# Sums of rows and edge products kept in PSUM, and pass 0's gathered rows copied there by ACT, in a graph network kernel

## The chip, the cores and the metric

The kernel runs on one core of one Trainium2 chip. The metric is the device time of one execution in microseconds; the figure for the kernel before is the median of three runs. Times that name a line come from one profiled execution of the kernel before.

The engines are named as in the profile: PE is TensorE, DVE is VectorE, ACT is ScalarE, POOL is GpSimd, and SP is SyncE, which here only issues DMAs. PEld is PE's loading of weights.

## The reference, cut to what matters

Two layers of a graph network over 6250 nodes with 256 features and 100000 edges. The edges are sorted by their destination. Everything is fp32.

```python
# layer 0
theta_x = (x[dst] - x[src]) @ theta_w.T + theta_b
phi_x   = x[src] @ phi_w.T + phi_b
out = segment_max(relu(theta_x + phi_x), dst)           # 0 where a node has no edge
x = layernorm(x + out)
# layer 1
hv = x @ W_in + b_in
for W, b in ((W_u0, b_u0), (W_u1, b_u1)):
    m   = relu(concatenate([hv[src], he], -1) @ W + b)    # he: 64 features per edge
    msg = segment_max(m, dst)
    hv  = where(has_in, msg + hv, hv)
x = layernorm(x + relu(hv @ W_ro + b_ro))
```

The theta term of x[dst] is the same for all edges of a node, so the maximum over the edges of a node needs only one row per edge that depends on the source. In layer 0 that row is x[src] @ (phi - theta); in layer 1 it is hv[src] @ W (upper part) plus he @ W (lower part).

## The kernel before, in words

A prologue in `gnn_kernel` makes the table of source rows of layer 0 in DRAM (L533 on PE, L536 on ACT). It also works out, in `check`, whether the destinations are sorted. They are, so the program takes the branch `in_order`.

`in_order` calls `sweep(r)` three times: pass 0 is layer 0, and passes 1 and 2 are the two rounds of layer 1. The edges lie in 17 blocks; in a block, each of the 128 partitions holds a run of consecutive edges (56 in most blocks). One step `s` handles one edge per partition, 128 edges, and a pass has `FS` = 782 steps. In each step:

- `sources` (L719, POOL) gathers the 128 source rows of 1 KB each from `table[r]` into a slice of the tile `run`, which holds K = 8 steps and has four buffers. It is issued 16 steps ahead (`AHEAD`).
- In passes 1 and 2, `pair` (L730, PE) multiplies the edge features of two steps by the lower part of the weights: two matrix products of 128x512 fp32 into one PSUM bank `hp`, one pair of steps ahead. Every second step the addition L923 (DVE) adds this bank to the two gathered rows in `run`. The edge features come by `features`, a DMA of ACT's queue every eight steps.
- L926 (DVE, `scalar_tensor_tensor`) carries the running maximum: the previous row, cut by `lim` where a new destination begins, against the current row, in place in `run`. A block's first row has no predecessor and is left as it is.
- Every eight steps SP stores the finished `run` tile to the DRAM tensor `S` (L932).

At the end of a block `over_lanes` carries the maxima from partition to partition: PE transposes (L741), ACT copies (L739, L758) and a DVE scan (L746).

A node's result is the row of `S` at its last edge, with what earlier partitions carry. This is done for tiles of 128 nodes, 49 in each pass, by `node(t, g, b)`. It is cut into small functions that `at` hangs on steps, called slots here. For each tile: `rows` gathers the rows of `S` (L771, POOL), `picks` (L783, DVE) and `carried` (L790, PE) bring what is carried. In pass 0 `theta` multiplies the tile of x (L700 and L702, PE, with the bank tag "he") at slot 8t+20, `theta_out` (L801, ACT) copies the product out at slot 8t+21, and `first_a` to `first_i` do the relu (L810, ACT), the layernorm (L682 is its square root, on ACT), the transposes (L692, PE, and their copy `aT`, L694, ACT), the products for the next pass and their copies (L830 and L834, ACT). Passes 1 and 2 have `next_a` to `next_d` and `last_d` to `last_g` at these places.

In the first part of pass 0 `count(c)` counts the edges of each node, at slot 3c+4 for c = 0 to 97: DVE compares the lower seven and the upper bits of the destinations of eight steps with a row of indices, which makes the one-hots `ol` (L647) and `oh` (L650), and PE multiplies them into `hist` (L653). The node stage of pass 0 begins when this is done, at slot 297.

The order on each engine is the order of the program text (`manual_schedule`): an engine executes its instructions in that order, and each waits for the data and buffers that it needs. [...]the tags "v", "pr", "he" and "tp" have two each.

Of the kernel before, what the change touches and what calls it, by code (L numbers as in the profile page):

```python
# [8 lines left out]
F32 = mybir.dt.float32  # L9
BF16 = mybir.dt.bfloat16  # L10
I32 = mybir.dt.int32
AF = mybir.ActivationFunctionType
OP = mybir.AluOpType
# [4 lines left out]
P = 128  # L18
N = 6250
D = 256  # L20
DE = 64
E = 100000
NT = 49
K = 8
# [12 lines left out]
FS = sum(BLOCKS)  # L37
# [396 lines left out]
def gnn_kernel(  # L434
# [3 lines left out]
    nc = tc.nc  # L438
    const = ctx.enter_context(tc.tile_pool(name="const", bufs=1))
# [32 lines left out]
    fd, pd, ld, nd = (ends_sb[:, i, :] for i in range(4))  # L472
    s_s = const.tile([P, FS], I32)
    whole = const.tile([P, NB], F32)
    lim = const.tile([P, FS], F32)
    breaks = const.tile([P, 1], I32)
    lo = const.tile([P, FS], BF16)
    hi = const.tile([P, FS], BF16)
    with tc.manual_schedule(), tc.tile_pool(name="pro", bufs=2) as pro, \
            tc.tile_pool(name="pro_ps", bufs=4, space=PSUM) as pps:  # L480
        wd = pro.tile([P, 2, D], F32, name="wd", bufs=1)
        wt = pro.tile([P, 2, D], F32, name="wt", bufs=1)
        nc.sync.dma_start(wd, ph_wT.rearrange("(k p) f -> p k f", p=P))
        nc.scalar.dma_start(wt, th_wT.rearrange("(k p) f -> p k f", p=P))
        dp = pro.tile([P, 2 * FS], I32, name="dp", bufs=1)
        d_s, p_s = dp[:, :FS], dp[:, FS:]
        parts = []
        for g in range(NT // PART):
            xg = pro.tile([P, 2, PART * P], F32, name="xg", bufs=NT // PART)
            nc.sync.dma_start(xg, xTn[:, :, g * PART * P:(g + 1) * PART * P])  # L490
            parts.append(xg)
            if g == 0:
                nc.sync.dma_start(dp, pos[:, 4 * NB:4 * NB + 2 * FS])
                nc.sync.dma_start(ends_sb.rearrange("p a b -> p (a b)"), pos[:, :4 * NB])
        nc.sync.dma_start(s_s, pos[:, 4 * NB + 2 * FS:])
        nc.vector.tensor_sub(wd, wd, wt)

        def check():
            down = pro.tile([P, FS], F32, name="down", bufs=1)
            nc.vector.tensor_tensor(down, p_s, d_s, OP.is_gt)  # L500
            downs = pro.tile([P, 1], F32, name="downs", bufs=1)
            nc.vector.tensor_reduce(downs, down, AX.X, OP.max)
            out_of = pro.tile([1, 2, NB], F32, name="out_of", bufs=1)
            nc.vector.tensor_tensor(out_of[:, 0, :], fd[0:1, :], floor, OP.is_lt)
            nc.vector.tensor_tensor(out_of[:, 1, :], fd[0:1, :], ceil, OP.is_gt)
            bad = pro.tile([1, 1], F32, name="bad", bufs=1)
            nc.vector.tensor_reduce(bad, out_of.rearrange("p a b -> p (a b)"), AX.X, OP.max)
            nc.vector.tensor_max(downs[0:1, :], downs[0:1, :], bad)
            breaks_p = pps.tile([P, 512], F32, name="breaks_p", bufs=1)
            nc.tensor.matmul(breaks_p[:, :1], every, downs, start=True, stop=True)  # L510
            nc.vector.tensor_copy(breaks, breaks_p[:, :1])
            keep = pro.tile([P, FS], F32, name="down", bufs=1)
            nc.vector.tensor_tensor(keep, p_s, d_s, OP.is_equal)
            alike = BLOCKS.count(BLOCKS[0])
            nc.vector.tensor_reduce(whole[:, :alike], keep[:, :alike * BLOCKS[0]].rearrange(
                "p (b s) -> p b s", s=BLOCKS[0]), AX.X, OP.min)
            for b in range(alike, NB):
                nc.vector.tensor_reduce(whole[:, b:b + 1], keep[:, FIRST[b]:FIRST[b] + BLOCKS[b]], AX.X, OP.min)
            nc.vector.tensor_scalar(lim, keep, 2.0 * BIG, -BIG, OP.mult, OP.add)
            bits = pro.tile([P, FS], I32, name="bits", bufs=1)  # L520
            nc.vector.tensor_scalar(bits, d_s, P - 1, None, OP.bitwise_and)
            nc.vector.tensor_copy(lo, bits)
            nc.vector.tensor_scalar(bits, d_s, 7, None, OP.arith_shift_right)
            nc.vector.tensor_copy(hi, bits)

        for g, xg in enumerate(parts):
            g0 = pro.tile([P, PART, D], F32, name="g0", bufs=3)
            for i in range(0, PART, 2):
                w = min(2, PART - i)
                ps = pps.tile([P, 512], F32, name="ps0")  # L530
                for q in range(w):
                    for k in range(2):
                        nc.tensor.matmul(ps[:, q * D:(q + 1) * D], xg[:, k, (i + q) * P:(i + q + 1) * P], wd[:, k, :],  # L533
                                         start=(k == 0), stop=(k == 1))
                put = g0[:, i:i + w, :].rearrange("p a f -> p (a f)")
                nc.scalar.copy(put, ps[:, :w * D])  # L536
            nc.sync.dma_start(table[0][g * PART * P:(g + 1) * PART * P, :].rearrange("(a p) f -> p a f", p=P), g0)
            if g == 0:
                check()
# [10 lines left out]
def in_order(ctx: ExitStack, tc: tile.TileContext, g):  # L550
# [5 lines left out]

    nc = tc.nc
    table, ident, above, every, col, col_f = (g[n] for n in ("table", "ident", "above", "every", "col", "col_f"))
    whole, lim, lo, hi, s_s, fd, pd, ld, nd = (g[n] for n in ("whole", "lim", "lo", "hi", "s_s", "fd", "pd", "ld", "nd"))
    heT, xTn, xn, out = (g[n] for n in ("heT", "xTn", "xn", "out"))  # L560
    ctx.enter_context(tc.manual_schedule())
    one = ctx.enter_context(tc.tile_pool(name="one", bufs=1))
# [75 lines left out]
        nc.vector.tensor_add(tb, tb, pb)  # L638


    hist = psum.tile([P, 512], F32, tag="v", name="hist")

    def count(c):
        k = min(K, FS - c * K)
        cut = slice(c * K, c * K + k)
        ol = work.tile([P, K, P], BF16, name="ol", bufs=1)
        nc.vector.tensor_tensor(ol[:, :k, :], col.unsqueeze(1).to_broadcast([P, k, P]),  # L647
                                lo[:, cut].unsqueeze(2).to_broadcast([P, k, P]), OP.is_equal)
        oh = work.tile([P, K, NT], BF16, name="oh", bufs=1)
        nc.vector.tensor_tensor(oh[:, :k, :], col[:, :NT].unsqueeze(1).to_broadcast([P, k, NT]),  # L650
                                hi[:, cut].unsqueeze(2).to_broadcast([P, k, NT]), OP.is_equal)
        for j in range(k):
            nc.tensor.matmul(hist[:, :NT], ol[:, j, :], oh[:, j, :], start=(c == 0 and j == 0),  # L653
                             stop=(c == NG - 1 and j == k - 1))

    cnt, incl, end = (one.tile([P, NT], F32, name=n) for n in ("cnt", "incl", "end"))
    sums = []
# [37 lines left out]
        return aT  # L695

    def times(aT, w, b, n, tag="pr"):
        ps = psum.tile([P, 512], F32, tag=tag, name="prod")
        for k in range(2):
            nc.tensor.matmul(ps[:, :n], aT[:, k, :], w[:, k, :], start=(k == 0), stop=(k == 1 and b is None))  # L700
        if b is not None:
            nc.tensor.matmul(ps[:, :n], every[0:1, :], b, start=False, stop=True)  # L702
        return ps

    def sweep(r):
# [20 lines left out]

        def pair(i):
            c, q = divmod(i, K // 2)
            hp[i] = psum.tile([P, 512], F32, tag="he", name="hp")
            nc.tensor.matmul(hp[i], hT[c][:, q, :], whe[r - 1].rearrange("p s f -> p (s f)"), start=True, stop=True)  # L730
            if q == K // 2 - 1:
                del hT[c]
# [30 lines left out]
        def node(t, g, b):  # L763

            n = min(P, N - t * P)
            N1 = D + 2 if r == 0 else D
            o = {}
# [17 lines left out]

            def carried():
                assert max(carried_in) - SPAN[t][0] < KEPT
                o["v"] = psum.tile([P, 512], F32, tag="v", name="v")
                for blk, p in o["pick"]:
                    nc.tensor.matmul(o["v"][:, :N1], p, cs[:, blk % KEPT, :N1], start=(blk == SPAN[t][0]),  # L790
                                     stop=(blk == SPAN[t][1]))
# [114 lines left out]
        for s in range(-AHEAD, FS):  # L906
# [5 lines left out]
            if r > 0:  # L912
                if s == 0:
                    for i in range(4):
                        features(i)
                    pair(0)
                elif j == 0 and c + 3 < NG:
                    features(c + 3)
                if s % 2 == 0:
                    if s + 2 < FS:  # L920
                        pair(s // 2 + 1)
                    two = runs[c][:, j:j + 2, :].rearrange("p s f -> p (s f)")
                    nc.vector.tensor_add(two, two, hp.pop(s // 2))  # L923
            cur = runs[c][:, j, :]
            if s > FIRST[blk]:
                nc.vector.scalar_tensor_tensor(cur, prev, lim[:, s:s + 1], cur, OP.min, OP.max)  # L926
            prev = cur
            if j == K - 1 or s in (FS - 3, FS - 1):
                k = 2 if s == FS - 1 else j + 1
# [62 lines left out]
```

## Time and profile before

| what | value |
|---|---|
| median of 3 runs | 4128.87 us (4111.4 to 4133.28) |
| profiled execution, whole | 4091.96 us |
| its span | 4090.2 us |
| mean granted TensorE clock | 0.667 |
| busy: PE, DVE, ACT, POOL | 50%, 51%, 7%, 60% |
| pass 0, its count part | about 130 to 503 us |
| pass 0, the rest | about 503 to 1390 us |
| pass 1 | about 1390 to 2710 us |
| pass 2 | about 2710 to 4010 us |

The parts of the span are read from the first and last gathers and one-hots of each. A row of the groups has the line, the engine, the operation, the tiles out<-in with their shape and the count; then the busy time in us and the mean duration in ns; then how long the engine was idle just before these instructions, and what ended most of that. "remote" means a semaphore for which the trace names no sender, and "issue" a time in which the engine waited for nothing that the profile shows. A row of the waits has the waiting engine and line, what it waited for, the total in us, how often, and the longest.

### The profile page before, as it was taken

To read this page: it belongs to the slowest core of one execution; us is meant where nothing else is said; L and a number is where in the kernel's file an instruction comes from. 1 tells how busy PE (TensorE), PEld (TensorE's weight loads), DVE (VectorE), ACT (ScalarE), POOL (GpSimd) and SP (SyncE) were. 2 spreads that over 40 slices of the span, in tenths; PEclk is the share of its full clock that TensorE was granted. 3 is DMA by queue.
4 is the path that set the end of the run, shared out by engine and by line. 5 is a ranking of instruction groups with operands and counts; after the bars stand their busy time and mean duration, and the time that the engine had idled before them with its cause. 6 is when DMAs were issued, how large, how long until landed. Compare 5 with 4: busy or idle time off the path is not lost.

```text
span 4090.2 us, 22048 instructions
## 1 busy us (share of the span) xinstructions
PE 2032.6 (50%) x4957; PEld 915.2 (22%) x4957; DVE 2083.0 (51%) x4526; ACT 280.7 (7%) x770; POOL 2459.6 (60%) x2499
## 2 busy tenths in 40 slices
PE   5433444232334745455464555664455545555557
PEld 4222222111112311111121222221121212122223
DVE  2766733433334555454554454545555555555555
ACT  1000010000101100000000000110000000000001
POOL 3777755666664466566666655546666666655542
PEclk7555565555555867676777777786766777777766
DMA  6755544454554456565555555545655555555542
GB/s 223 250 195 181 195 157 169 166 181 161 170 168 147 147 189 211 172 205 179 195 192 184 181 181 183 172 164 191 204 191 193 191 180 192 182 174 171 175 146 86
DMA packets 237763, 735.87 MB, mean 180 GB/s; under 512 B 51880, under 2 KB 91799, under 8 KB 200375
## 3 DMA queue, kind: packets, MB, share of 16 engines
q0 software_dynamic: 119664, 326.92, 26.7%
q1 hardware_dynamic: 66096, 334.71, 21.5%
q10 hardware_dynamic: 51862, 72.75, 5.4%
q8 instruction: 42, 0.69, 0.1%
q14 instruction: 99, 0.80, 0.1%
HBM read 401.01 MB, written 333.16 MB: 179 GB/s over the span
## 4 chain that ended last, share of the span: by engine, by line
another core or an unknown queue 31%; DVE 18%; PE 16%; issue 15%; POOL 9%; DMA 8%; ACT 1%; ACTq 0%; DVEq 0%; POOLq 0%; SPq 0%
POOL run L719 9%; DVE run L926 8%; DVE run L923 7%; DMA run<-table,s_s 5%; PE hp L730 5%; PE prod L700 4%; PE prod L702 2%; PE v L790 2%; DMA S<-run 1%; PE ps L533 1%; PE tp L692 1%; ACT aT L694 1%; DVE pick L783 1%; DMA hT<-in_heT 0%
## 5 line engine op out<-in xcount | busy, mean ns | idle before, releaser
L719 POOL DMA_INDIRECT run<-table,s_s x2346 | 2316.6, 987 | 1294.2 <-issue 696.2
L730 PE MATMUL hp<-whe,hT 128*128 128x512 f32 x1564 | 1054.5, 779 | 589.7 <-DVE run L923 378.2
L926 DVE SCALAR_TENSOR_TENSOR run<-run,lim 128x256 f32<-128x256 f32 x2295 | 1110.6, 484 | 205.7 <-DMA run<-table,s_s 120.5
L923 DVE TENSOR_TENSOR run<-run,hp 128x512 f32<-128x512 f32 x782 | 533.7, 682 | 809.0 <-remote 459.7
L730 PEld LDWEIGHTS hp<-whe,hT 128*128 128x128 f32 x1564 | 308.0, 233 | 1190.7 <-DVE run L923 699.6
L771 POOL DMA_INDIRECT m<-S,end_i x147 | 142.4, 969 | 291.6 <-DMA S<-run 191.4
L700 PE MATMUL prod<-wcat,aT 128*128 128x256 f32 x392 | 160.4, 550 | 261.9 <-ACT aT L694 167.6
L790 PE MATMUL v<-cs,pick 128*128 128x256 f32 (+1 forms) x468 | 192.6, 540 | 123.9 <-DVE pick L783 70.9
L692 PE MATMUL tp<-ident,h_sb 128*128 128x128 f32 x196 | 52.7, 361 | 358.9 <-DVE h_sb L841 223.6
L653 PE MATMUL hist<-oh,ol 128*128 128x49 bf16 x782 | 48.8, 217 | 249.2 <-DVE oh L650 182.2
L700 PEld LDWEIGHTS prod<-wcat,aT 128*128 128x128 f32 x392 | 95.5, 268 | 314.2 <-ACT aT L694 177.6
L790 PEld LDWEIGHTS v<-cs,pick 128*128 128x128 f32 x468 | 116.2, 272 | 199.6 <-issue 83.5
L746 DVE TENSOR_TENSOR_SCAN cT<-lim,cT,lp 128x128 f32<-128x128 f32 x96 | 40.8, 468 | 218.5 <-PE lp L741 144.5
L853 DVE SCALAR_TENSOR_TENSOR m<-prod,x_sb 128x256 f32<-128x256 f32 x49 | 20.8, 424 | 248.9 <-remote 169.9
L700 PE MATMUL prod<-wro,aT 128*128 128x256 f32 x196 | 90.4, 609 | 96.8 <-issue 76.1
L647 DVE TENSOR_TENSOR ol<-col,lo 128x1024 bf16<-128x1024 bf16 x98 | 119.3, 1217 | 26.3 <-remote 25.7
L692 PEld LDWEIGHTS tp<-ident,h_sb 128*128 128x128 f32 x196 | 25.1, 173 | 451.4 <-issue 318.5
L741 PE MATMUL lp<-ident,run 128*128 128x128 f32 x102 | 28.7, 375 | 183.0 <-ACT lim L739 101.5
L700 PE MATMUL prod<-wu,aT 128*128 128x256 f32 x196 | 75.6, 524 | 68.4 <-ACT aT L694 36.7
L837 DVE TENSOR_TENSOR m<-m,v 128x256 f32<-128x256 f32 x98 | 40.5, 414 | 134.9 <-remote 78.1
L653 PEld LDWEIGHTS <-ol 128*128 128x128 bf16 x782 | 42.8, 117 | 276.2 <-DVE ol L647 164.5
L700 PE MATMUL prod<-th,xT 128*128 128x256 f32 x196 | 95.5, 640 | 8.8 <-issue 8.8
(116 smaller groups left out, 1326.0 us busy)
## 6 DMA issues: line engine op xcount, KB each, us to landing
S<-run SPq DMA_DIRECT2D x291, 1024.0 KB
hT<-in_heT ACTq DMA_DIRECT2D x196, 256.0 KB
run<-table,s_s POOLq DMA_INDIRECT x2346
table<-new ACTq DMA_DIRECT2D x98, 128.0 KB
xg<-in_xTn SPq DMA_DIRECT2D x7, 896.0 KB
table<-g SPq DMA_DIRECT2D x7, 896.0 KB
xT<-in_xTn SPq DMA_DIRECT2D x49, 128.0 KB
x_sb<-in_xn SPq DMA_DIRECT2D x7, 896.0 KB
```

The lines of the kernel that those rows point to most:

```text
L533: nc.tensor.matmul(ps[:, q * D:(q + 1) * D], xg[:, k, (i + q) * P:(i + q + 1) * P], wd[:, k, :], start=(k == 0), stop=(k == 1))
L647: nc.vector.tensor_tensor(ol[:, :k, :], col.unsqueeze(1).to_broadcast([P, k, P]), lo[:, cut].unsqueeze(2).to_broadcast([P, k, P]), OP.is_e ...
L653: nc.tensor.matmul(hist[:, :NT], ol[:, j, :], oh[:, j, :], start=(c == 0 and j == 0), stop=(c == NG - 1 and j == k - 1))
L692: nc.tensor.transpose(tp[:, k * P:(k + 1) * P], a[:, k * P:(k + 1) * P], ident)
L700: nc.tensor.matmul(ps[:, :n], aT[:, k, :], w[:, k, :], start=(k == 0), stop=(k == 1 and b is None))
L702: nc.tensor.matmul(ps[:, :n], every[0:1, :], b, start=False, stop=True)
L719: nc.gpsimd.indirect_dma_start(out=runs[s // K][:, s % K, :], out_offset=None, in_=table[r], in_offset=bass.IndirectOffsetOnAxis(ap=s_s[:, ...
L730: nc.tensor.matmul(hp[i], hT[c][:, q, :], whe[r - 1].rearrange("p s f -> p (s f)"), start=True, stop=True)
L771: i = nc.gpsimd.indirect_dma_start(out=o["m"], out_offset=None, in_=S_r[:P * (FIRST[SPAN[t][1]] + BLOCKS[SPAN[t][1]]), :], in_offset=bass. ...
L790: nc.tensor.matmul(o["v"][:, :N1], p, cs[:, blk % KEPT, :N1], start=(blk == SPAN[t][0]), stop=(blk == SPAN[t][1]))
L923: nc.vector.tensor_add(two, two, hp.pop(s // 2))
L926: nc.vector.scalar_tensor_tensor(cur, prev, lim[:, s:s + 1], cur, OP.min, OP.max)
```

## The change

- The lower and upper bits of the destinations go into one tile `bits_sb`. `count` has ACT copy the bits of its eight steps to a PSUM tile (tag "pr"), and the two comparisons read them there.
- `hist` and `v` share one bank in place of two. The tag "he" (theta's product, `hp` and the new `rows`) has three banks in place of two.
- In passes 1 and 2 `pair` is issued two pairs ahead in place of one. The addition writes its sums over the product in PSUM; the running maximum reads the previous row from SBUF and the current one from PSUM, and writes to `run`. A block's first row is copied from PSUM to `run` (34 copies on DVE).
- In pass 0 ACT copies each two gathered rows to PSUM, 391 copies of 128x512 fp32, and the running maximum reads them there.

ACT gets 489 instructions more and DVE 34; POOL and SP have the same instructions in the same order. In ACT's order the copy of the rows of an even step stands ahead of the functions that hang on this step and behind those of the steps before.

```diff
@@ -474,8 +474,7 @@
     whole = const.tile([P, NB], F32)
     lim = const.tile([P, FS], F32)
     breaks = const.tile([P, 1], I32)
-    lo = const.tile([P, FS], BF16)
-    hi = const.tile([P, FS], BF16)
+    bits_sb = const.tile([P, 2, FS], BF16)
     with tc.manual_schedule(), tc.tile_pool(name="pro", bufs=2) as pro, \
             tc.tile_pool(name="pro_ps", bufs=4, space=PSUM) as pps:
         wd = pro.tile([P, 2, D], F32, name="wd", bufs=1)
@@ -519,9 +518,9 @@
             nc.vector.tensor_scalar(lim, keep, 2.0 * BIG, -BIG, OP.mult, OP.add)
             bits = pro.tile([P, FS], I32, name="bits", bufs=1)
             nc.vector.tensor_scalar(bits, d_s, P - 1, None, OP.bitwise_and)
-            nc.vector.tensor_copy(lo, bits)
+            nc.vector.tensor_copy(bits_sb[:, 0, :], bits)
             nc.vector.tensor_scalar(bits, d_s, 7, None, OP.arith_shift_right)
-            nc.vector.tensor_copy(hi, bits)
+            nc.vector.tensor_copy(bits_sb[:, 1, :], bits)
 
         for g, xg in enumerate(parts):
             g0 = pro.tile([P, PART, D], F32, name="g0", bufs=3)
@@ -556,7 +555,7 @@
 
     nc = tc.nc
     table, ident, above, every, col, col_f = (g[n] for n in ("table", "ident", "above", "every", "col", "col_f"))
-    whole, lim, lo, hi, s_s, fd, pd, ld, nd = (g[n] for n in ("whole", "lim", "lo", "hi", "s_s", "fd", "pd", "ld", "nd"))
+    whole, lim, bits_sb, s_s, fd, pd, ld, nd = (g[n] for n in ("whole", "lim", "bits_sb", "s_s", "fd", "pd", "ld", "nd"))
     heT, xTn, xn, out = (g[n] for n in ("heT", "xTn", "xn", "out"))
     ctx.enter_context(tc.manual_schedule())
     one = ctx.enter_context(tc.tile_pool(name="one", bufs=1))
@@ -638,17 +637,18 @@
         nc.vector.tensor_add(tb, tb, pb)
 
 
-    hist = psum.tile([P, 512], F32, tag="v", name="hist")
+    hist = psum.tile([P, 512], F32, tag="v", name="hist", bufs=1)
 
     def count(c):
         k = min(K, FS - c * K)
-        cut = slice(c * K, c * K + k)
+        bits = psum.tile([P, 2, K], F32, tag="pr", name="bits")
+        nc.scalar.copy(bits[:, :, :k], bits_sb[:, :, c * K:c * K + k])
         ol = work.tile([P, K, P], BF16, name="ol", bufs=1)
         nc.vector.tensor_tensor(ol[:, :k, :], col.unsqueeze(1).to_broadcast([P, k, P]),
-                                lo[:, cut].unsqueeze(2).to_broadcast([P, k, P]), OP.is_equal)
+                                bits[:, 0, :k].unsqueeze(2).to_broadcast([P, k, P]), OP.is_equal)
         oh = work.tile([P, K, NT], BF16, name="oh", bufs=1)
         nc.vector.tensor_tensor(oh[:, :k, :], col[:, :NT].unsqueeze(1).to_broadcast([P, k, NT]),
-                                hi[:, cut].unsqueeze(2).to_broadcast([P, k, NT]), OP.is_equal)
+                                bits[:, 1, :k].unsqueeze(2).to_broadcast([P, k, NT]), OP.is_equal)
         for j in range(k):
             nc.tensor.matmul(hist[:, :NT], ol[:, j, :], oh[:, j, :], start=(c == 0 and j == 0),
                              stop=(c == NG - 1 and j == k - 1))
@@ -695,7 +695,7 @@
         return aT
 
     def times(aT, w, b, n, tag="pr"):
-        ps = psum.tile([P, 512], F32, tag=tag, name="prod")
+        ps = psum.tile([P, 512], F32, tag=tag, name="prod", bufs=3 if tag == "he" else 2)
         for k in range(2):
             nc.tensor.matmul(ps[:, :n], aT[:, k, :], w[:, k, :], start=(k == 0), stop=(k == 1 and b is None))
         if b is not None:
@@ -726,7 +726,7 @@
 
         def pair(i):
             c, q = divmod(i, K // 2)
-            hp[i] = psum.tile([P, 512], F32, tag="he", name="hp")
+            hp[i] = psum.tile([P, 512], F32, tag="he", name="hp", bufs=3)
             nc.tensor.matmul(hp[i], hT[c][:, q, :], whe[r - 1].rearrange("p s f -> p (s f)"), start=True, stop=True)
             if q == K // 2 - 1:
                 del hT[c]
@@ -785,7 +785,7 @@
 
             def carried():
                 assert max(carried_in) - SPAN[t][0] < KEPT
-                o["v"] = psum.tile([P, 512], F32, tag="v", name="v")
+                o["v"] = psum.tile([P, 512], F32, tag="v", name="v", bufs=1)
                 for blk, p in o["pick"]:
                     nc.tensor.matmul(o["v"][:, :N1], p, cs[:, blk % KEPT, :N1], start=(blk == SPAN[t][0]),
                                      stop=(blk == SPAN[t][1]))
@@ -914,16 +914,25 @@
                     for i in range(4):
                         features(i)
                     pair(0)
+                    pair(1)
                 elif j == 0 and c + 3 < NG:
                     features(c + 3)
-                if s % 2 == 0:
-                    if s + 2 < FS:
-                        pair(s // 2 + 1)
-                    two = runs[c][:, j:j + 2, :].rearrange("p s f -> p (s f)")
-                    nc.vector.tensor_add(two, two, hp.pop(s // 2))
+            if s % 2 == 0:
+                two = runs[c][:, j:j + 2, :].rearrange("p s f -> p (s f)")
+                if r > 0:
+                    if s + 4 < FS:
+                        pair(s // 2 + 2)
+                    sums = hp.pop(s // 2)
+                    nc.vector.tensor_add(sums, sums, two)
+                else:
+                    sums = psum.tile([P, 512], F32, tag="he", name="rows", bufs=3)
+                    nc.scalar.copy(sums, two)
             cur = runs[c][:, j, :]
+            row = sums[:, s % 2 * D:(s % 2 + 1) * D]
             if s > FIRST[blk]:
-                nc.vector.scalar_tensor_tensor(cur, prev, lim[:, s:s + 1], cur, OP.min, OP.max)
+                nc.vector.scalar_tensor_tensor(cur, prev, lim[:, s:s + 1], row, OP.min, OP.max)
+            elif r > 0:
+                nc.vector.tensor_copy(cur, row)
             prev = cur
             if j == K - 1 or s in (FS - 3, FS - 1):
                 k = 2 if s == FS - 1 else j + 1
```

## The prediction

> **What bounds the kernel now.** I read the busy shares first, then the groups, then tables by stretch, then the waits.
>
> ```profile
> PE 2032.6 (50%) x4957; PEld 915.2 (22%) x4957; DVE 2083.0 (51%) x4526; ACT 280.7 (7%) x770; POOL 2459.6 (60%) x2499
> L719 POOL DMA_INDIRECT run<-table,s_s x2346 | 2316.6, 987 | 1294.2 <-issue 696.2
> L730 PE MATMUL hp<-whe,hT 128*128 128x512 f32 x1564 | 1054.5, 779 | 589.7 <-DVE run L923 378.2
> L926 DVE SCALAR_TENSOR_TENSOR run<-run,lim 128x256 f32<-128x256 f32 x2295 | 1110.6, 484 | 205.7 <-DMA run<-table,s_s 120.5
> L923 DVE TENSOR_TENSOR run<-run,hp 128x512 f32<-128x512 f32 x782 | 533.7, 682 | 809.0 <-remote 459.7
> ```
>
> No engine is full. POOL has the most: 2346 gathers of rows, with an idle "issue" of 696.2/2346 = 0.30 us behind each. One gather uninterrupted takes a median of 0.946 us (next fence), so a row costs POOL 0.946 + 0.30 = 1.25 us, and its 2493 gathers (2346 and the 147 of L771) at least 3116 us of the 4090. DVE needs 0.48 us per row in pass 0, and (0.68 + 2 x 0.48)/2 = 0.82 in passes 1 and 2. **POOL is thus the clock wherever nothing stops it**, and the rest is stops.
>
> ```profile
> L719 POOL DMA_INDIRECT run<-table,s_s x2346: 940/946/2422, 59.9 to 4006.4; - x196
> ```
>
> The mean, 0.987, lies above the median, so some gathers are lengthened. The table of L719 by stretch (times, POOL busy, count, TensorE clock, DMA share, GB/s) says where: the count stretch of pass 0, the rest of pass 0, pass 1, pass 2.
>
> ```profile
> 130.00:503.00 373.00, 287.05 (x252) 0.50 0.63 209
> 503.00:1390.00 887.00, 464.71 (x484) 0.57 0.48 161
> 1390.00:2710.00 1320.00, 759.24 (x782) 0.73 0.56 185
> 2710.00:4010.00 1300.00, 755.14 (x782) 0.71 0.55 184
> ```
>
> 287.05/252 = 1.139 us in the count stretch. Above 0.946 each, that is 49, 7, 19 and 15 us; with the prologue **97 us in all, 2.4% of the span: the most that freeing POOL can return**. The waits of DVE and ACT:
>
> ```profile
> DVE run L923 <- PE hp L730: 117.7, 68, 8.2
> DVE run L923 <- remote: 459.7, 104, 20.7
> ACT h_sb L801 <- PE prod L702: 306.0, 34, 40.2
> ```
>
> The sums wait 117.7 us for the edge product by name and 459.7 for something the trace doesn't name. ACT, 7% busy, waits at L801 with nothing behind it.
>
> **What the Trainium skill says.** "SBUF — State Buffer", section "Who interferes with whom": VectorE and GpSimd share a port pair under an exclusive lock, which a VectorE instruction with two SBUF inputs takes against a GpSimd one that reads SBUF. The trace agrees in part: gathers lengthen most (1.139) beside the one-hots and the running maximum, both with two SBUF inputs, while the latter keeps its 484 ns. "PSUM — Partial Sum Buffer", section "Specifications (TRN2)": VectorE and ScalarE may write 4-byte types to PSUM, ScalarE faster than to SBUF; a VectorE instruction takes at most one tensor from PSUM. The change keeps to it; no run here shows such a write yet. "ScalarE: Activation LUTs", section "What ACT_TABLE_LOAD costs": 186 ns + 0.833 per element of a lane, 612 ns at 512; the trace's 128x512 copies (L536) took 586, which I use.
>
> **The change part by part.**
>
> *Running maximum from PSUM (all passes).* L926 keeps one SBUF row and takes the other from PSUM. The same operation from PSUM at L806 takes 484 ns, as L926 does: 0 on DVE. For POOL it takes away the second SBUF input. L923 keeps one (the gathered rows) and now writes PSUM: between -0.06 and +0.06 us x 782 = 47 us of DVE time; I take +5, since POOL, needing 2.5 us per pair against DVE's 1.64, hides most. If that cover is gone, all 47 count.
>
> *34 copies of each block's first row, passes 1 and 2.* At the 0.41 us of a 128x256 addition (L837), 14 us; half where DVE is late: +7.
>
> *Third "he" bank, product two pairs ahead.* The matmuls are the same. It allows PE one more pair of lead, against the 117.7 us. Between 0 and -118; I take a fifth, -24, as most late pairs come where PE itself is behind for several pairs.
>
> *"v" and "hist" down to one bank.* The next `carried` stands five slots or more behind `first_a`'s reading: 0.
>
> *98 copies of the bits on ACT.* 16 values a lane, 0.2 us as the small copy L749 (196 ns), ahead of use: 0 in themselves, but they queue on ACT like the rows.
>
> *391 copies of two rows on ACT, pass 0.* 391 x 0.586 = 229 us on an engine with 16 us busy of 373 and 103 of 887: its time is free, **its order is not**. ACT executes as written. A pair's copy now stands behind `theta_out`, the relu L810, the root L682, `aT` L694 and the copies L830/L834, and the running maximum waits for it. Before, DVE passed all of these. Around one theta the timeline shows
>
> ```profile
> 204.51 0.56 DVE L650 TENSOR_TENSOR oh<-col,hi 128x392 bf16<-128x392 bf16 x1
> ...
> 205.44 2.06 PE L700 MATMUL prod<-th,xT 128*128 128x256 f32 x4
> ...
> 207.43 1.22 PE L702 MATMUL prod<-tb,every 1*128 1x256 f32 x2
> ...
> 208.55 0.48 DVE L926 SCALAR_TENSOR_TENSOR run<-run,lim 128x256 f32<-128x256 f32 x1
> ...
> 208.68 0.37 ACT L801 COPY h_sb<-prod 128x256 f32<-128x256 f32 x1 [12.88 <-PE prod L702]
> ```
>
> The theta matmuls stand on PE behind the histogram of the one-hots that end at 205.07; L801 starts 3.61 us later. Add 0.37 for it and 0.59 for the rows of slot 8t+22: 4.57 us from the one-hots to the next running maximum that DVE may do. What DVE has in between depends on which slot the count falls: two slots of row work or less (0.48 or 0.97), or 1.45 and the next count (1.22 + 0.56). Idle 4.1, 3.6 or 1.3 us, each once in three thetas, 24 slots: 9.0 us. DVE is busy 272.85 us for the 272 rows of this stretch, 24.1 per 24: with the idle 33.1, or 1.38 us a row. Today's rate is 373/272 = 1.37, and POOL without contention would allow 1.25. So the relief of 49 us is taken back by ACT's order, and where the two don't mesh more is lost. Bounds: -33 (POOL alone the clock, (1.37 - 1.25) x 272) and +65 (1.61 a row: all 9.0 us of idle on top of 1.25, less a third); I take 1.46, **+25**.
>
> At each of 49 nodes of pass 0 the relu and the rows behind it (0.51 + 0.59, less 0.48 of DVE's work) cost 0.6 us, and the transposes (2 x 0.36), `aT` (0.37) and the rows (0.59) less 0.48 another 1.2; with the hand-offs 2.1 us, 103 in all. Where POOL is the clock its rows lie ahead and hide it: 0 to 103, half taken, **+50**. The other rows get back some of 7 us: -4.
>
> *Passes 1 and 2.* ACT's order is untouched there. Relief of the 34 us: six tenths, as the rest falls where POOL stops anyway: -20.
>
> Sum: +25 + 50 - 4 - 20 - 24 + 7 + 5 = **+39 us**. The profiled execution took 4091.96 us (span 4090.2 and 1.8 around it), 0.9% below the median of 4128.87, so the sum gives 4131 in its terms and 4168 against the median.
>
> **The rivals.**
>
> *A, the likeliest: pass 0 waits for ACT in order.* As above, 4168; with its bounds 4120 to 4260.
>
> *B, faster: POOL stays the clock and is freed.* The gathers run 16 rows ahead, and if this lead swallows ACT's waits the count stretch falls to 1.25 a row: -33. Passes 1 and 2 give -20, the product's lead a third of 118: -40, the first rows +7: -86, or 4043; with the node stage and the nameless waits improved also, 4000. It decides where DVE's idle per 24 slots stays under 24 x 1.25 - 24.1 = 5.9 us; I worked out 9.0, not far off. For it: POOL's share, the highest, and the lengthened gathers. Against it: 9.0 is over 5.9, and the node stage has no relief to set against its waits.
>
> *C, no change.* The relief and the waits cancel: 4129. The bounds of the count stretch alone allow it.
>
> *D, much slower.* In parts of passes 1 and 2 the sums come every 5.6 us instead of 2.5, and by their own rows neither DVE nor PE (2.08 us of matmul) accounts for it:
>
> ```profile
> 2867.43 0.69 DVE L923 TENSOR_TENSOR run<-run,hp 128x512 f32<-128x512 f32 x1 [3.87 <-remote]
> ...
> 2873.03 0.69 DVE L923 TENSOR_TENSOR run<-run,hp 128x512 f32<-128x512 f32 x1 [3.87 <-issue]
> ```
>
> I count 127 such intervals of 781. If sums that PSUM must hold longer, or a PE that runs further ahead, make that state commoner by half, 64 x 3.1 us = +200: 4330. If rarer by half, 3930. Nothing in the profile says which.
>
> **How the numbers follow.** A 0.42, B 0.38, C 0.12, D 0.08 (its slow side). Half a per cent, 20.6 us, is about what a measurement of this kernel can tell from no change. Faster by more: B, 0.38. Within: 0.12, with A's low end in it. Slower: A and D, 0.50. The time is that of A, 4168. The range, 4000 to 4300, takes in B down to its own bound and A whole, and leaves out most of D.
>
> **What would show it.** For A: gathers in the count stretch near 0.95 us, yet the stretch no shorter than 373 us, with DVE L926 waiting for ACT's rows, and ACT L801's wait for PE now on the path; passes 1 and 2 shorter by 20 to 60 us together; the node stage of pass 0 longer by some 50. B shows a count stretch of 340 us and POOL with few stops. A relief that is not there (gathers still 1.1 us beside one-hots read from PSUM) would leave A's waits alone and go higher. The forecast is wrong if passes 1 and 2 move by over 100 us either way: then the nameless waits have moved.

## The result, and the profile after

The changed kernel takes 4260.45 us (median of 4 runs, 4250.86 to 4275.72) against 4130.49 for the kernel before (median of four, one run more than in the table above): a ratio of 1.0328 with a 95% interval of 1.0284 to 1.0372. Forecast was 4168. The direction was right and the size was not, by a factor of over three (+130 us, where +39 was forecast).

The page of the changed kernel, busy shares and groups (L926 is now the addition, L933 the running maximum, L929 ACT's copy of the rows):

```profile
PE 2039.8 (48%) x4957; PEld 909.9 (21%) x4957; DVE 2090.1 (49%) x4560; ACT 499.6 (12%) x1259; POOL 2359.7 (55%) x2499
L719 POOL DMA_INDIRECT run<-table,s_s x2346 | 2219.8, 946 | 1525.9 <-issue 722.3
L926 DVE TENSOR_TENSOR hp<-hp,run 128x512 f32<-128x512 f32 x782 | 543.5, 695 | 626.6 <-remote 357.5
L933 DVE SCALAR_TENSOR_TENSOR run<-run,lim,rows 128x256 f32<-128x256 f32 x765 | 365.8, 478 | 687.7 <-ACT rows L929 456.7
L929 ACT COPY rows<-run 128x512 f32<-128x512 f32 x391 | 226.5, 591 | 119.2 <-DMA run<-table,s_s 44.9
```

The relief of POOL is there to the last microsecond: the mean gather fell from 987 to 946 ns, 2316.6 to 2219.8 us, which is the forecast bound of 97. Yet the time rose, and POOL's idle time before its gathers with it, from 1294.2 to 1525.9. The groups show one new wait, 456.7 us of DVE for ACT's rows; some 144 us of it lie in the count stretch, the rest behind it.

The same table of L719 by stretch, at the changed kernel's own boundaries:

```profile
130.00:617.00 487.00, 260.79 (x276) 0.50 0.51 167
617.00:1545.00 928.00, 440.84 (x466) 0.54 0.46 152
1545.00:2885.00 1340.00, 739.75 (x783) 0.72 0.55 182
2885.00:4190.00 1305.00, 738.53 (x781) 0.72 0.56 182
```

The count stretch went from 373 to 487 us, the rest of pass 0 from 887 to 928, passes 1 and 2 from 1320 and 1300 to 1340 and 1305. So 114 us of the loss lie where 49 us of POOL's time were given back. TensorE's granted clock in the count stretch is 0.50 in both tables. These are single executions; the run e6 below, which has the change in passes 1 and 2 alone, shows no difference there.

In the timeline of the changed kernel an ordinary theta and a late one stand close together. The late one first:

```profile
335.81 2.05 PE L700 MATMUL prod<-th,xT 128*128 128x256 f32 x4
337.79 1.22 PE L702 MATMUL prod<-tb,every 1*128 1x256 f32 x2
348.20 0.37 ACT L801 COPY h_sb<-prod 128x256 f32<-128x256 f32 x1 [17.29 <-remote]
348.47 0.60 ACT L929 COPY rows<-run 128x512 f32<-128x512 f32 x1
...
349.10 0.48 DVE L933 SCALAR_TENSOR_TENSOR run<-run,lim,rows 128x256 f32<-128x256 f32 x1 [12.75 <-ACT rows L929]
...
357.72 2.05 PE L700 MATMUL prod<-th,xT 128*128 128x256 f32 x4
359.70 1.22 PE L702 MATMUL prod<-tb,every 1*128 1x256 f32 x2
360.96 0.37 ACT L801 COPY h_sb<-prod 128x256 f32<-128x256 f32 x1 [8.61 <-PE prod L702]
...
361.85 1.00 DVE L933 SCALAR_TENSOR_TENSOR run<-run,lim,rows 128x256 f32<-128x256 f32 x2 [4.11 <-ACT h_sb L801]
```

By its own rows PE has done both thetas 3.2 us after their start. ACT, idle and waiting, gets the second after 3.24 us and the first only after 12.39. DVE waits 4.11 us behind the second, as forecast for that alignment, and 12.75 behind the first, where 3.6 was forecast for its alignment. I call a theta late where the interval from its first row to ACT's copy is over 3.6 us: 1 of 35 in the kernel before, 7 of 35 in the changed one.

The rows of PE don't show when its results were done, but the trace also has the moments at which semaphores are counted up. Taken in order, the histogram ahead of the ordinary theta and the theta itself count at 357.66, 357.91, 359.79 and 360.93 us, close behind their rows. Around the late theta the same four counts come at 340.37, 343.22, 346.77 and 348.18, and ACT starts 0.02 us after the last. So it is PE that is late, not ACT, and its lateness begins in the histogram ahead of the theta. Neither a missing input nor the clock accounts for it: the late theta's tile of x had landed at 325.3 us, and the granted clock was 0.50 without a break from 56 to 653 us, through late and ordinary thetas alike.

### The profile page after: what moved, and what is told of

The parts are those of the page before. It is cut to its first block, busy times and chain, and to the rows that moved or that the text cites. A ratio compares the mean times of both kernels' runs of the same rounds, so it can differ in the third digit from the quotient of the medians.

```text
span 4273.4 us, 23381 instructions
## 1 busy us (share of the span) xinstructions
PE 2039.8 (48%) x4957; PEld 909.9 (21%) x4957; DVE 2090.1 (49%) x4560; ACT 499.6 (12%) x1259; POOL 2359.7 (55%) x2499
## 4 chain that ended last, share of the span: by engine, by line
issue 16%; another core or an unknown queue 14%; DVE 14%; PE 12%; POOL 5%; DMA 3%; ACT 1%; POOLq 0%; ACTq 0%; DVEq 0%; SPq 0%
DVE hp L926 7%; DVE run L933 6%; PE hp L730 5%; POOL run L719 5%; PE prod L700 3%; PE prod L702 2%; DMA run<-table,s_s 1%; PE v L790 1%; DMA S<-run 1%; PE tp L692 1%; DMA hT<-in_heT 1%; ACT aT L694 0%; DVE cT L746 0%; DVE pick L783 0%
## 5 line engine op out<-in xcount | busy, mean ns | idle before, releaser
L719 POOL DMA_INDIRECT run<-table,s_s x2346 | 2219.8, 946 | 1525.9 <-issue 722.3
L926 DVE TENSOR_TENSOR hp<-hp,run 128x512 f32<-128x512 f32 x782 | 543.5, 695 | 626.6 <-remote 357.5
L933 DVE SCALAR_TENSOR_TENSOR run<-run,lim,hp 128x256 f32<-128x256 f32 x1530 | 733.2, 479 | 49.4 <-DVE run L933 1.8
L933 DVE SCALAR_TENSOR_TENSOR run<-run,lim,rows 128x256 f32<-128x256 f32 x765 | 365.8, 478 | 687.7 <-ACT rows L929 456.7
L929 ACT COPY rows<-run 128x512 f32<-128x512 f32 x391 | 226.5, 591 | 119.2 <-DMA run<-table,s_s 44.9
L700 PE MATMUL prod<-wcat,aT 128*128 128x256 f32 x392 | 178.6, 603 | 79.8 <-issue 41.0
L837 DVE TENSOR_TENSOR m<-m,v 128x256 f32<-128x256 f32 x98 | 40.8, 416 | 314.4 <-remote 209.2
L692 PE MATMUL tp<-ident,x_sb 128*128 128x128 f32 x98 | 30.5, 410 | 291.6 <-issue 99.3
L647 DVE TENSOR_TENSOR ol<-col,bits 128x1024 bf16<-128x1024 bf16 x98 | 118.8, 1212 | 58.1 <-remote 46.0
L838 ACT ACTIVATE m<-m,has 128x256 f32<-128x256 f32 x98 | 49.7, 507 | 633.7 <-issue 256.6
L694 ACT COPY aT<-tp 128x256 f32<-128x256 f32 x147 | 54.7, 372 | 560.2 <-remote 250.3
```

The costliest lines, as they stand in the source:

```text
L692: nc.tensor.transpose(tp[:, k * P:(k + 1) * P], a[:, k * P:(k + 1) * P], ident)
L719: nc.gpsimd.indirect_dma_start(out=runs[s // K][:, s % K, :], out_offset=None, in_=table[r], in_offset=bass.IndirectOffsetOnAxis(ap=s_s[:, ...
L926: nc.vector.tensor_add(sums, sums, two)
L929: nc.scalar.copy(sums, two)
L933: nc.vector.scalar_tensor_tensor(cur, prev, lim[:, s:s + 1], row, OP.min, OP.max)
```

## The experiments

Two theories. **Order**: DVE waits because ACT executes as written, with the rows and bits behind theta's copy, the relu and the rest. **Pace**: gathers that come too closely, as they do once POOL is freed, make PE late, and whatever waits for PE is late with it. In the expectations they are also called theory 1 and theory 2. Ratios are to the kernel before on the same chip; its median was 4096 to 4125 us in the four sets of runs. Stage times are from one profile each, the count stretch from its first to its last one-hot: 432 us before, 547 changed. Single profiles scatter: e6, with pass 0 as before except for one PSUM bank, has 445.

### Undoing parts

**e1_no_rows.** Pass 0's maximum reads SBUF again; the bits still go through ACT and PSUM.

```diff
-                    sums = psum.tile([P, 512], F32, tag="he", name="rows", bufs=3)
-                    nc.scalar.copy(sums, two)
+                    sums = two
```

> The changed kernel, but pass 0's running maximum reads the gathered rows in SBUF, without ACT's 391 copies; bits, sums of passes 1 and 2 and banks stay as changed. Theory 'ACT's order in pass 0': the 115 us of the count stretch and most of the 39 of the node stage are gone, so 4100 to 4140 us. Rival 'the sums in PSUM and the bank that v lost cost as much': 4170 to 4220 us.

Measured: 1.0231 (1.0194 to 1.0268), 4191 us, which is in the rival's range; e6 below speaks against that rival. The count stretch is 554 us, no shorter. The node stage is: 869 us from the last one-hot to pass 1, against 928 changed and 889 before. DVE now waits at the one-hots: from 130 us to the end of the stretch 73 us for the bits, which stand behind theta's copy as the rows did, and 98 for an unnamed sender. Both theories' waits remain, so this run doesn't separate them; it shows that the rows aren't the whole cause.

**e2_pass0_only.** Passes 1 and 2 as before.

```diff
-                    sums = hp.pop(s // 2)
-                    nc.vector.tensor_add(sums, sums, two)
+                    sums = two
+                    nc.vector.tensor_add(two, two, hp.pop(s // 2))
```

> The changed kernel with passes 1 and 2 as before (sums in SBUF, product one pair ahead). Theory 'ACT's order in pass 0': it keeps the whole loss, 4240 to 4270 us, and passes 1 and 2 take what they take before (1320 and 1300) within 20 us. Rival 'passes 1 and 2 share in it': 4190 to 4220 us.

Measured: 1.0305 (1.0263 to 1.0348), 4214 us. The ratio is the whole loss, within the intervals. (The absolute time lies in the rival's range because the kernel before took 4096 us on this chip.) Pass 1 took 1331 us, against 1320 before.

**e6_passes12_only.** The counterpart: pass 0 as before, only the sums in PSUM, the third bank and the pair two ahead.

> The changed kernel with pass 0 as before: bits and rows in SBUF; only the sums in PSUM, the third bank and the product two pairs ahead are left, and one bank for v and hist. Theories 1 and 2 alike put the loss into pass 0: within 20 us of the kernel before, the count stretch 432 us. Rival 'the sums in PSUM cost as much as they give, or more': slower by 30 to 60 us, in passes 1 and 2.

Measured: 0.9986 (0.9962 to 1.0010). No loss and no gain, although the gathers of passes 1 and 2 are freed there too (a mean of 948 ns, 968 before). The loss is pass 0's. As `hist` and `v` share one bank here as well, that bank isn't its cause.

**e3_theta_out_later** and **e4_rows_ahead.** Two ways to take the rows out from behind theta's copy.

```diff
-                at(8 * t + 21, theta_out)
+                at(8 * t + 24, theta_out)
```

```diff
+                    for i in range(s // 2 + (2 if s else 0), min(s // 2 + 3, FS // 2)):
+                        hp[i] = psum.tile([P, 512], F32, tag="he", name="rows", bufs=3)
+                        nc.scalar.copy(hp[i], <rows of pair i>)
+                    sums = hp.pop(s // 2)
```

> The changed kernel with ACT's copy of theta's product at slot 8t+24 in place of 8t+21, so that the rows of slots 8t+22 and 8t+24 stand ahead of it. Theory 'ACT's order in pass 0': DVE's waits of 3.6 and 4.1 us behind each theta go and most of the late ones shrink, the count stretch falls from 487 to 390 to 420 us, the time to 4160 to 4190 us. Rival 'PE itself is late there, and DVE then waits at the next histogram': the count stretch stays above 450 us, the time above 4220 us.

> The changed kernel with pass 0's rows copied two pairs ahead in ACT's order (theta's product in tag tp, so that the three banks hold rows alone). Theory 'ACT's order in pass 0': the waits at theta go as in the run before, and those at relu, root and aT in the node stage too, so 4120 to 4170 us. Rival 'copying itself is the cost, wherever it stands': 4230 to 4260 us.

Measured: 1.0163 (1.0113 to 1.0213) and 1.0211 (1.0177 to 1.0244), 4164 us without one execution of 4215, and 4180. Each gives back half of the loss at most. The time of e3 is that of Order, but its count stretch is 525 us with 15 of 35 thetas late, as the rival has it; its one profile is of the execution of 4215 us. The time of e4 lies between its two forecasts. Its node stage went back to 882 us, as Order says; the count stretch stayed at 551, with 93 us of waits for the bits, which had not been moved, and 10 of 35 thetas late.

**e5_bulk_bits.** Here no one-hot and no row stands behind theta's copy: rows in SBUF, the bits of 32 counts copied at a time, passes 1 and 2 as before. (Not shown: the one bank of `hist` and `v`.)

```diff
+        if c % 32 == 0:
+            n = min(32 * K, FS - c * K)
+            held[:] = [psum.tile([P, 2, 32 * K], F32, tag="bits", name="bits", bufs=1)]
+            nc.scalar.copy(held[0][:, 0, :n], lo[:, c * K:c * K + n])
+            nc.scalar.copy(held[0][:, 1, :n], hi[:, c * K:c * K + n])
+        bits = held[0][:, :, c % 32 * K:c % 32 * K + k]
```

> The kernel before, but the one-hots read the bits from PSUM, where ACT puts 32 counts' bits at a time (8 copies in place of 98, so that no one-hot stands behind theta's copy); v and hist have one bank; rows stay in SBUF. Theory 1, 'ACT's order delays DVE': there is no such order here, POOL is freed, and the count stretch falls from 432 to 390 to 410 us, the time by 20 to 40 us. Theory 2, 'gathers at their full pace make PE late, and the one-hots wait for the histogram': the count stretch grows to 470 us or more with DVE waiting at L647 for an unnamed sender, and the time by 40 to 100 us.

Measured: 1.0166 (1.0130 to 1.0203), count stretch 512 us, 15 of 35 thetas late. DVE's waits at the one-hots (wait, total in us, times, longest):

```profile
DVE ol L654 <- remote: 138.1, 23, 17.3
```

and a stretch of its timeline:

```profile
302.89 1.22 PE L709 MATMUL prod<-tb,every 1*128 1x256 f32 x2
310.27 1.22 DVE L654 TENSOR_TENSOR ol<-col,bits 128x1024 bf16<-128x1024 bf16 x1 [8.30 <-remote]
311.06 0.37 ACT L808 COPY h_sb<-prod 128x256 f32<-128x256 f32 x1 [18.68 <-remote]
```

The one-hots have one buffer, so they wait for PE to have read the last ones; theta's copy, for which nothing in this stretch waits here, comes as late. PE's counts agree: one comes at 310.25 us, and the one-hot starts 0.02 us later. This kernel freed POOL's gathers (0.959 us on the average in this stretch, 1.129 before), added eight copies to an idle ACT, and lost 1.7%. ACT's order cannot explain it.

### The pace by itself

**e7_paced.** To the kernel *before* an operation is added that does nothing but occupy POOL.

```diff
+            nc.gpsimd.iota(scratch, pattern=[[1, P]], base=0, channel_multiplier=0)
             nc.gpsimd.indirect_dma_start(
                 out=runs[s // K][:, s % K, :], out_offset=None, in_=table[r],
```

> The kernel before with an index operation of 128x128 (about 0.2 us) on POOL ahead of each gather of rows, its result unused: gathers come every 1.45 us at best instead of 1.25. Theory 2: PE is late less often, the intervals of 4.5 to 6.5 us between sums fall from 127 to under 60, and the time stays within 40 us or falls, although POOL has 470 us more to do. Theory 'POOL is the clock wherever nothing stops it': slower by 200 to 400 us.

Measured: 0.9684 (0.9619 to 0.9749), 3977 us. From its trace, the operation and what is left of the unnamed wait at the sums (459.7 us before):

```profile
L721 POOL IOTA scratch<- 128x128 int32 x2346 | 589.0, 251 | 73.1 <-remote 26.0 <-issue 23.3 <-POOL scratch L721 0.6
DVE run L926 <- remote: 267.2, 67, 14.5
```

POOL got 589 us of useless work, and the kernel gained over 3%. POOL's stops of some length in passes 1 and 2 (gathers more than 4 us apart) went from 57 to 25; no theta was late. The intervals of 4.5 to 6.5 us between sums fell from 127 to 65, a little less than expected. The gain lies behind the count stretch, which at 441 us is no shorter.

**e8_bulk_bits_paced.** The same operation in e5, ahead of the first 297 gathers alone.

> The kernel with 32 counts' bits in PSUM at a time, and the same index operation ahead of the first 297 gathers alone. Theory 2: the paced gathers leave PE on time, DVE's waits at L647 for an unnamed sender fall below 30 us and the count stretch is back at 430 to 460 us. If PE's lateness has nothing to do with POOL's pace, the count stretch is that of the unpaced kernel or longer.

Measured: 1.0018 (0.9990 to 1.0047): 1.5% better than e5. But the expectation of Pace failed. The count stretch is 494 us (512 in e5), 17 of 35 thetas are late (15 in e5), and DVE's wait at the one-hots has not fallen:

```profile
DVE ol L655 <- remote: 144.0, 32, 12.4
```

The single profiles put only 18 us of the gain into this stretch. With the gathers freed this operation makes 1.37 us between them; the kernel before has a mean of 1.45 in this stretch (its stops left out), with no such operation. So 1.37 may be too fast still; this run alone doesn't show that the pace is what counts here.

**f1_paced256, f4_paced448** are e7 with wider operations; **f2_after_paced128, f3_after_paced256** and **h1_after_paced192** the changed kernel with them. The diff is that of e7 with another width.

> The kernel before with an index operation twice as wide (128x256) ahead of each gather: gathers every 1.5 us at best. Theory 2, 'gathers at their full pace make PE late': the intervals of 4.5 to 6.5 us between sums fall further, from 65 with the narrow operation to under 30, and the time is 3900 to 3980 us. If the narrow operation helped by something other than the slower pace, or POOL becomes the clock at this pace: 4000 to 4100 us.

> The changed kernel with the narrow index operation (128x128) ahead of each gather. Theory 2: the late thetas and late sums go, while the regular waits of DVE for ACT behind each theta (3.6, 4.1 and 1.4 us, 107 us in the count stretch) stay: 1 to 2% faster than the changed kernel loses now, so 4020 to 4090 us, slower than the paced kernel before by 60 to 110. If ACT's order were not a cost of its own: within 30 us of the paced kernel before.

> The changed kernel with the wide index operation (128x256) ahead of each gather. Theory 2: no late theta is left, DVE's waits behind theta are the regular ones alone, the count stretch 470 to 500 us, the time 4000 to 4080 us.

> The kernel before with an index operation of 128x448 ahead of each gather, gathers every 1.7 us at best. Here POOL must be the clock: 2346 x 1.7 + 147 x 1.25 = 4170 us of POOL's time alone, so 4250 to 4350 us, with no interval of 4.5 to 6.5 us left between sums (under 10).

> The changed kernel with an index operation of 128x192 ahead of each gather, between the two widths run (4017 us at 128x128, 3845 at 128x256): gathers every 1.42 us at best. If the lateness of PE sets in below this pace, POOL is the clock and the time is 3845 - 2346 x 0.05 = 3730 us; if it sets in above, 3900 to 3960 us.

The last three columns are from one profile each: DVE's wait for an unnamed sender at the sums (us), the late thetas of 35, and the count stretch (us). h2 is described below.

| kernel | median spacing of gathers, us | time, us | ratio (interval) | unnamed wait | late | count |
|---|---|---|---|---|---|---|
| changed | 1.25 | 4260 | 1.0328 (1.0284 to 1.0372) | 357.5 | 7 | 547 |
| f2, changed, 128x128 | 1.37 | 4018 | 0.9777 (0.9727 to 0.9826) | 163.1 | 4 | 492 |
| h1, changed, 128x192 | 1.43 | 3966 | 0.9624 (0.9549 to 0.9700) | 96.9 | 8 | 477 |
| h2, changed, fill | 1.44 | 3849 | 0.9348 (0.9280 to 0.9416) | 11.3 | 7 | 475 |
| f3, changed, 128x256 | 1.47 | **3845** | **0.9372 (0.9333 to 0.9411)** | none | 0 | 434 |
| before | 1.25 | 4096 to 4125 | 1 | 459.7 | 1 | 432 |
| e7, before, 128x128 | 1.37 | 3977 | 0.9684 (0.9619 to 0.9749) | 267.2 | 0 | 441 |
| f1, before, 128x256 | 1.48 | 3943 | 0.9603 (0.9556 to 0.9651) | none | 0 | 463 |
| f4, before, 128x448 | 1.64 | 4298 | 1.0483 (1.0440 to 1.0526) | none | 0 | 525 |

Slower gathers, shorter time, until POOL really is the clock; f4 lies beyond that point. The unnamed wait at the sums goes down with the pace, step by step. The late thetas don't go down as evenly, but those of h1 and h2 take 5.3 us at most, where the changed kernel has up to 12.39.

f3 takes as long as h2, within the noise, and less than both kernels and all others. Its table of gathers by stretch, beside those of the two kernels above:

```profile
130.00:507.00 377.00, 241.40 (x256) 0.50 0.59 197
507.00:1317.00 810.00, 457.69 (x481) 0.57 0.53 177
1317.00:2564.00 1247.00, 740.43 (x783) 0.71 0.59 196
2564.00:3775.00 1211.00, 740.17 (x781) 0.70 0.60 199
```

In the count stretch POOL is now the clock: 256 gathers at 1.47 us are 376 us of the 377. Against the changed kernel every stretch is shorter, at nearly the same granted clock (0.50 in the count stretch again); against the kernel before, the count stretch is what it was and the gain lies behind it. The waits of DVE, ACT and POOL in f3:

```profile
DVE hp L928 <- DMA run<-table,s_s: 792.6, 460, 11.5
DVE run L935 <- ACT rows L931: 491.0, 212, 38.7
DVE hp L928 <- PE hp L732: 73.5, 44, 2.8
...
ACT rows L931 <- DMA run<-table,s_s: 348.8, 136, 6.0
...
POOL run L721 <- issue: 371.1, 2253, 1.9
```

DVE has no wait for an unnamed sender left, where L926 alone had 357.5 us; it waits for gathers, directly or through ACT's copies, which themselves wait for gathers, and POOL waits 1.9 us at most in its large group (25.0 in the changed kernel). No theta is late, and the count stretch is 434 us with every one of ACT's 489 copies in place. f1 and f4 missed in one point: the intervals of 4.5 to 6.5 us between sums are still 101 and 103, but now DVE waits for gathers there and for no unnamed sender, so this count had stopped measuring PE's lateness. f3 did much better than expected, and f2 a little, though four late thetas are left in it: I had put 107 us of regular waits behind theta on top, and in f3, where DVE waits for the gathers anyway, they cost nothing. h1, 6 us above its range, fell on the side of a later onset: there PE is still late at times.

**h2_after_memset256.** Another operation in place of the index operation.

```diff
+            nc.gpsimd.memset(scratch, 0.0)
```

> The changed kernel with a fill of 128x256 on POOL in place of the index operation. If the pace is what counts, the time follows the pace that the fill makes: at 1.45 to 1.55 us per gather 3820 to 3960 us, with hardly a stop of POOL. If it was something about the index operation, the time is that of the changed kernel unpaced, 4230 us or more.

Measured: 0.9348 (0.9280 to 0.9416), 3849 us, median spacing 1.44 us, as expected of the pace. The gain doesn't hang on the index operation.

**h3_after_bursts.** Eight operations in a row after every eight gathers.

```diff
+            for _ in range(K if s % K == 0 else 0):
+                nc.gpsimd.iota(scratch, pattern=[[1, 256]], base=0, channel_multiplier=0)
```

> The changed kernel with the same index operations of 128x256, but eight in a row after each eight gathers, so that the mean pace stays and the gathers come in bursts at 1.25 us. If the pace of several gathers in a row makes PE late, the gain is lost in part: 3950 to 4150 us, with late thetas again. If the mean pace alone counts: within 40 us of 3845.

Measured: 1.0379 (1.0300 to 1.0458), 4277 us. Both expectations missed. No theta was late and no large wait for PE was left, so bursts of eight at 1.25 us, with a stop behind each, don't make PE late. But the mean pace did not stay: eight gathers took 13.3 us, 1.66 each, since between gathers the operation uses part of the 0.30 us of issue and in a row it doesn't. At 1.66 POOL alone makes it slow, as in f4.

## Why the prediction was wrong, by its steps

*Contention and its bound of 97 us.* Right in size (96.8) and **wrong in worth: this is the step that failed**. The sum had the relief as a gain or as nothing, the +25 of the count stretch being ACT's order with the relief set against it. In the count stretch it went with a loss: 432 to 512 us in e5, which has the relief and no order. The lengthened gathers had been a brake there, at 1.45 us a gather, near the 1.47 at which f3 shows PE on time. The changed kernel lets go of it, and f3, with all of the change and gathers at 1.47 us, has the old count stretch back (434). That the brake alone kept PE on time is argued from this and not tested by itself: no run has the traffic of the kernel before with faster gathers only. Reading PSUM for the bits and rows could add to PE's lateness, but isn't enough for it: f3 and h3 read there too and have no late theta.

What the change is worth depends on the pace. At 1.47 to 1.48 us a gather it gains 98 us (f3 3845, f1 3943); at 1.37 it loses 41 (f2 4018, e7 3977). These are the whole change; the relief's share in them wasn't measured.

*"POOL is the clock wherever nothing stops it."* The groups and the shares suggested it, and e7 refutes it for the kernel before: POOL with 589 us more to do makes a shorter time. I had read the stops of POOL as the thing to shorten, not as the end of a stretch in which it ran too fast.

*Rival D.* It named the late PE, at a chance of 0.08, and looked for it in passes 1 and 2. The late PE was there in the kernel before, as e7's gain shows; the loss of the change came in pass 0, where the kernel before showed a single late theta.

*ACT's order.* The waits were 3.60, 4.11 and 1.43 us for the three alignments in the trace, where I had 3.6, 4.1 and 1.3. The working that put them together failed: I added 9.0 to DVE's busy 24.1 and left out the idle time that no gather explains. Of DVE's 100 us idle in the old stretch (373.00 less 272.85) 36 were waits for gathers, and some 64 were not; had they stayed, the order would have given 273 + 64 + 102 = 439 us in place of 373, +66 and not +25. The bound of +65 doesn't follow from its words: all 9.0 us on top of 1.25 make 1.63 a row, and a third less 1.50, not 1.61. In the end, as PE was late too, the order is the smaller part: 547 us with it against 512 without, some 35, though the runs don't add up so neatly, as one wait hides the other.

*Node stage of pass 0.* +50 was forecast. Measured 889 to 928, +39, in one profile each. Single profiles scatter here by as much (e5 850 and e6 881 with this stage as before), but those with rows behind relu and `aT` have 908 to 928 (e2, e3, changed) and those without have 850 to 889 (before, e1, e4, e5, e6). Right as far as that shows.

*Passes 1 and 2.* -32 forecast, 0.9986 measured, -6 us with an interval of -16 to +4. The wait for `hp` by name fell from 117.7 to 90.8, about the 24 that I took, but e6, with the same passes, has 121.5, so that this gain isn't shown. The unnamed wait at the sums fell from 459.7 to 357.5, while that at L837, where a node's maximum meets what is carried, rose from 78.1 to 209.2: the lateness moved. POOL's relief became other stops: its gathers in these passes wait 266 us for DVE's sums and maxima in place of 229 (315 in e6). The new operations cost what was said: 695 ns for the addition into PSUM (682), 424 for a first-row copy (0.41), 591 for a rows copy (0.586).

Open is how the pace makes PE late. Its rows show no longer matmuls, only its semaphores come late, and the granted clock doesn't differ. In h3 eight gathers at 1.25 us, with a stop behind them, do no harm; no run shows more of the mechanism.

## What to carry to other kernels

When an engine off the critical path is made faster, ask what its slower pace had been protecting; to add a small delay to it is a cheap experiment, and here it was worth more than the change. A bound on a gain, such as "97 us of contention", says nothing of a loss. And a wait that the trace can't name (460 us at one line here) should widen a forecast in both directions, in every stretch, before anything is built on the waits that it does name.

## What the runs showed of the hardware

Indirect gathers of 128 rows of 1 KB, issued back to back from POOL at 1.25 us each, go together with results of PE that come long after PE's own rows say that they are done: 9.2 us in the theta shown (348.20 against 337.79 + 1.22), at a granted clock of 0.50 before, during and after. With 1.47 us between them (f3) no late theta and no unnamed wait at the sums is left; with 1.44 (h2) 11.3 us of the latter and seven thetas late by 2.1 us at most, with a fill in place of an index operation. The copy of 128x512 fp32 by ACT took 591 ns from SBUF to PSUM and 586 from PSUM to SBUF; as source and destination change together, what PSUM as destination is worth can't be read from the two.
